# A four-layer graph kernel: half of the zero counts in the second attention loop, ten run-ahead steps stored in mask halves, diagonals and means in another order

## The chip, the cores and the metric

The kernel runs on one core of a Trainium2 chip. The core has a matrix engine (PE), a vector engine (DVE), an activation engine (ACT), a general engine (POOL), and an engine that here only issues transfers (SP). The metric is the device time of one execution, in microseconds, as the median over runs. Beside it stand one profiled execution and its span, from its first to its last instruction.

## The reference

Four residual layers follow one another on 3327 nodes of 64 features, with one 0/1 adjacency matrix of about 0.5 % ones:

```python
h = relu(layernorm(x)); x = x + L0(h, adj)   # hyperbolic attention
h = relu(layernorm(x)); x = x + L1(h, adj)   # decay sum
h = relu(layernorm(x)); x = x + L2(h, adj)   # signed attention with two GRU cells
h = relu(layernorm(x)); x = x + L3(h, adj)   # hyperbolic attention

# L0, L3: adj_att = sigmoid(left + right.T) * adj
#         support = einsum('ij,ijd->id', adj_att, logmap(x_i, x_j)), then expmap and proj
# L1:     rank = cumsum(adj != 0, axis=1); deg = rank[:, -1:]; k = min(deg, 100)
#         pos = rank - (deg - k)
#         out = (mask * where(pos > 0, 0.5 ** (k - pos), 0)) @ (h @ weight) + bias
# L2:     A = adj without its diagonal
#         edge = gru([(A > 0) @ h, (A < 0) @ h], h)
#         node = gru(gat(h, A, A), h)
#         out = diag(adj) * edge + diag(adj) * node
```

In L1 a neighbour counts by how many neighbours stand to its right in the row, so each block of the matrix needs counts before its sum can be made. L2 needs degrees without the diagonal.

## The kernel before

The nodes are padded to 3328, 26 blocks of 128. The matrix lies transposed in memory as f32. The kernel turns it into fp8 masks, thirteen tiles `mask` of two blocks each, and these stay on chip from the first loop to the end. A "quarter" k (0 to 51) is one column half c = k // 26 of one row block b = 25 − k % 26, 128 × 1664 values. Quarters are the unit of loads, masks and zero counts.

The fast path is only right for a matrix of zeros and ones. Therefore each quarter is also read for its zeros (`zeros`, L1335: one DVE instruction that compares with zero and accumulates the result into a column of `zo`). The counts of zeros and ones together must give 3328². The sum of `zo` goes into `ok` (L1964), and after everything else a slow path is taken if the total is wrong.

**First attention (layer 0) and second attention (layer 3), `hyperbolic_series`, L335.** 104 tiles of 1024 or 768 columns are gone through in pairs, index j in a loop at L682. For one tile PE makes two products (L609, L610), ACT takes an arctangent (L615) and a sigmoid (L596), POOL multiplies with the adjacency (L598: in the first loop from f32 as it is loaded, in the second from the masks), DVE makes the weights (L619), PE sums (L628, L636). In the first loop the class `Ahead` (L1316) adds to each j from 2 to 49 one DVE instruction on 128 × 832 values: either half a mask (L1326) or half a zero count (L1335), for quarters 0 to 11 (`EARLY` = 12), with their loads. The second loop has nothing of this kind.

**Decay sum (layer 1), `plain_decay`, L1360.** It goes through the quarters as 52 steps. For a step PE makes counts from the mask (L1437), ACT turns them into weights (`weights`, L1443, an exponential, 128 × 832 at a time, two a step), and PE makes the sums with the two fp16 parts of the features (L1451). The features only become known when the first attention has been finished off on DVE and ACT: `factors` (L709 and after; its tanh is L748, first used at L749), then a layer norm by four groups of blocks (`norms`, L1490 to L1525). During that time counts and weights of the steps 0 to `LAG` − 1 run ahead (`ahead_of_norm`, L1579), with the weights kept in places that are free: halves of masks not yet made, three own tiles and two spare load buffers. Then the loop from L1633 makes the sums of the steps that ran ahead (catching up, at most two sums a step) and counts and weights of the rest.

Masks of the quarters 12 to 51 are made here: `make_mask` (L1421) on DVE for some (L1423) and as a cast on POOL for others (L1426). `check` (L1428) makes the zero count for the quarters that are not in `LATE`, and then issues the load of a further quarter into the buffer that has become free (L1411, on SP). In program order the checks of quarters 16 and later come after the norms.

**Signed attention and GRU (layer 2), `plain_gat`, L1716.** PE goes through 26 blocks (L1738, 16 matmuls each), accumulating in four banks. Between them stand: the last part of layer 1's output (`last_x`, L1269 on PE, addition L1464 on DVE), the layer norm of its last blocks (`finish`, L1545 to L1572), transposes of the features (`turn`, L1774, with five ACT copies each), the diagonal's part of the degrees (`diagonal`, L1786, product L1790, subtraction on DVE L1803), the inverse of the degrees (`inverse`, L1805, ACT and DVE), and a product of weight matrices (`weights2`, L1765). Which of these follows which block is written down in the table `todo`. The nine zero counts of `LATE` are also here, with their own loads (L1753). After the last block the GRU takes the sums out of PSUM (`take`, L1837: ACT copies L1840, DVE multiplication by the inverse degrees L1841) and goes through eight steps (two cells, four column groups) of products, sigmoids and tanhs. An output bank is one half of a PSUM slot; four slots `cnt[0]`, `cnt[1]`, `acc[0]`, `acc[1]` give the banks 0 to 7.

[...]

Of the kernel before, what the change touches and what calls it, by code (L numbers as in the profile page):

```python
# [17 lines left out]
I32 = mybir.dt.int32  # L18
PSUM = bass.MemoryType.PSUM

N = 3327
P = 128
T = 26
# [25 lines left out]
def tile_gnn4(ctx: ExitStack, tc: tile.TileContext, x, adjT, att0, b0, w1, bias1, w_gat, a_gat,  # L49
# [285 lines left out]
    def hyperbolic_series(r, params, ok, masks=None, done=None, ahead=None, then=None):  # L335
# [18 lines left out]
        with ExitStack() as st:  # L354
# [12 lines left out]
            if ahead is not None:  # L367
                ahead.begin(pers)
            lp = st.enter_context(ExitStack())
# [312 lines left out]
            for j in range(-1, K // 2 + (5 if then is None else 1)):  # L682
                for k in (2 * j - 2, 2 * j - 1):
                    if 0 <= k < K:
                        sums(k)
                for i in range(2):
                    k = 2 * j + i
                    products(2 * j + 3 + i)
                    if 0 <= k < K:
                        weights(k)  # L690
                    if i == 0 and (j, 0) in later:
                        later.pop((j, 0))()
                    products(2 * j + 4)
                    if k + 2 < K:
                        angle(k + 2)
                    if k + 3 < K:
                        if masks is None and k + 5 < K:
                            load(k + 5)
                        sigmoid(k + 3)
                    if i == 1 and (j, 1) in later:  # L700
                        later.pop((j, 1))()
                if at(2 * j + 10, 1):
                    columns(at(2 * j + 10, 1))
                if ahead is not None:
                    ahead.step(j)
                if then is not None and j == K // 2 - 1:
                    table_of(AF.Exp)
# [566 lines left out]
    BY_V = range(EARLY + 7, 2 * T - 4, 4)  # L1274
    LATE = *range(EARLY, EARLY + 4), *BY_V[:2], *BY_V[5:]

# [56 lines left out]

    def zeros(same, adj, count):
        V.tensor_scalar(same, adj, 0.0, 0.0, op0=OP.is_equal, op1=OP.add, accum_out=count)  # L1335
# [24 lines left out]
    def plain_decay(e, right, masks, zo, wt, bias, gru, ball_of_r, then):  # L1360
# [8 lines left out]
        LAG = 12  # L1369
# [6 lines left out]
        with ExitStack() as st:  # L1376
# [13 lines left out]
            def in_mask(k, q):  # L1390
                return masks[k].bitcast(BF)[:, q, :].rearrange("p (o h i) -> p o h i", o=2, h=2)

            def in_adj(t, q):
# [3 lines left out]
            places = [in_mask(k, q) for k in (4, 3, 2, 1, 0) for q in range(2)] + own + [  # L1397
                in_adj(t, q) for t in spares for q in range(2)] + [in_mask(0, 0)]

            def place(k):  # L1400
                return places[k] if k < LAG + 6 else in_adj(spares[0], 0) if k == LAG + 9 else own[k % 3]

# [18 lines left out]
            def make_mask(k):  # L1421
                if k in (EARLY, EARLY + 1, EARLY + 4, EARLY + 5, EARLY + 6) or k in BY_V:
                    V.tensor_scalar(mask_of(masks, k), adjs[k], 1.0, None, op0=OP.is_equal, saturate=False)  # L1423
                else:

                    G.tensor_copy(mask_of(masks, k), adjs[k], saturate=False)  # L1426

            def check(k):  # L1428
                if k not in LATE:
                    zeros(same, adjs[k], zo[:, k:k + 1])  # L1430
                buf = adjs.pop(k)
                if k < T + 9 or not any(buf is t for t in ah_.own):
                    load(next(coming), buf)

# [148 lines left out]
            for k in range(EARLY, EARLY + 4):  # L1583
                make_mask(k)
            for k in range(EARLY, EARLY + 4):
                check(k)
# [3 lines left out]
            for k in range(4):  # L1590
                ahead_of_norm(k)
            ah, am = e.factors(tp)
            for k in range(4, LAG):
# [3 lines left out]
            def norms():  # L1597
# [9 lines left out]
                make_mask(EARLY + 4)  # L1607
                rest_of(normed(g, xs[2]))
                make_mask(EARLY + 5)
# [5 lines left out]
                make_mask(EARLY + 6)  # L1615
                centre(groups[3])
                make_mask(EARLY + 7)
# [15 lines left out]
            for k in range(LAG, K_ + 1):  # L1633
# [29 lines left out]
                if k in (LAG + 9, LAG + 11):  # L1663
                    load(next(coming), spares[(LAG + 11 - k) // 2])
                if k == LAG + 5:
                    for i in range(EARLY + 4, k + 1):
                        check(i)
                if EARLY + 8 <= k + LEAD < K_:
                    make_mask(k + LEAD)
                if LAG + 5 <= k < K_ - 1:  # L1670
# [45 lines left out]
    def plain_gat(masks, zo, deg, first, wg, gru, H, parts, banks, last_x, finish, close):  # L1716
# [8 lines left out]
        with ExitStack() as st:  # L1725
# [15 lines left out]

            block(0)
            last_x(0)
            block(1)
# [4 lines left out]
            wk = st.enter_context(room(name="pgl", bufs=4))  # L1749
            late = []  # L1750
            for k in LATE:
                late.append(wk.tile([P, 2, CW], F32, name="adj"))
                nc.sync.dma_start(late[-1], quarters(k))  # L1753
# [8 lines left out]
            for _ in range(1):  # L1762
                before = st.enter_context(ExitStack())
                tp = before.enter_context(room(name="pgn", bufs=1))
                def weights2():  # L1765
                    pt = bank(4)
                    PE.transpose(pt[:D, :D], wg, ident[:D, :D])
                    A.activation(wgT, pt[:D, :D], AF.Copy)
                    pt = bank(5)
# [4 lines left out]
                def turn(t0):  # L1774

                    n = min(4, C2 - t0)
                    pt = bank(4 + t0 // 4 % 2)
# [8 lines left out]
                def diagonal(k):  # L1786

                    dg = bank(6 + k % 2)[:, :BK]
                    for o in range(2):
                        PE.matmul(dg[o * D:(o + 1) * D, :], ones_bf[:, :D],  # L1790
                                  diag[:, o * HP + k * BK:o * HP + (k + 1) * BK], start=True, stop=True)
                    return dg

                def check(n=1):
                    for _ in range(n):
                        same = wk.tile([P, 2, CW], BF, name="same", bufs=1)
                        k = LATE[len(LATE) - len(late)]
                        zeros(same, late.pop(0), zo[:, k:k + 1])

                def degrees(*ks):  # L1800
                    for k in ks:
                        cs = slice(k * BK, (k + 1) * BK)
                        V.tensor_sub(deg[:, cs], deg[:, cs], diagonal(k))  # L1803

                def inverse():  # L1805

                    few, r0 = [tp.tile([P, HP], F32, name=n) for n in ("few", "r0")]
                    V.tensor_scalar(zo[:, 2 * T:2 * T + 2], zo[:, 2 * T:2 * T + 2], first, None, op0=OP.mult)
# [5 lines left out]
                    check(3)  # L1814
                    V.scalar_tensor_tensor(deg, deg, -1.0, r0, op0=OP.mult, op1=OP.mult)
                    V.scalar_tensor_tensor(deg, deg, 2.0, r0, op0=OP.add, op1=OP.mult)
                    check(len(late))


                todo = {11: lambda: (turn(0), check(3)), 12: lambda: degrees(0, 1), 13: lambda: turn(4),  # L1820
                        15: lambda: turn(8), 16: lambda: degrees(2, 3), 17: lambda: (turn(12), inverse()),
                        21: weights2}
# [14 lines left out]
                def take(k):  # L1837
                    cs = slice(k * BK, (k + 1) * BK)
                    for o in range(2):
                        A.activation(xh[0][o][:D, cs], acc[k][o * D:(o + 1) * D, :], AF.Copy, scale=1.0 / SH)  # L1840
# [60 lines left out]
                take(0)  # L1901
                for u in range(K + 2):
                    if u < K:
                        products(u)
                    if u == 0:
                        take(1)
                    if u < K:
                        sigmoids(u)
                    if u == 0:
                        take(2)  # L1910
                        take(3)
# [24 lines left out]
    zo = const.tile([P, 2 * T + 2 + EARLY], F32, name="zo")  # L1936
# [4 lines left out]
    with ExitStack() as ms:  # L1941
# [22 lines left out]
        V.reduce_sum(ok[:, 1:2], zo, axis=AX.X)  # L1964
        rs.close()
        mid.close()
        hyperbolic_series(r3, params3, ok[:, 2:3], masks, store)
# [57 lines left out]
```

## Time and profile before

| | us |
|---|---|
| median of 3 runs | 750.83 |
| lowest, highest | 748.64, 752.13 |
| profiled execution | 747.64 |
| its span | 745.9 |
| mean granted PE clock | 0.951 of full speed |

Busy time by part of the program, from the profile (stretch in us, busy us of PE, DVE, ACT and POOL, granted clock of PE, GB/s moved):

| stretch | PE | DVE | ACT | POOL | clock | GB/s |
|---|---|---|---|---|---|---|
| 250–275, decay, run-ahead | 23.15 | 17.91 | 22.28 | 0.00 | 0.94 | 72 |
| 275–300, decay, norms | 22.60 | 23.05 | 12.83 | 1.70 | 0.93 | 35 |
| 300–316, decay | 11.82 | 10.32 | 5.54 | 7.27 | 0.79 | 259 |
| 316–370, decay | 52.72 | 49.82 | 42.23 | 43.82 | 1.00 | 327 |
| 370–393, decay, end | 20.33 | 15.90 | 15.63 | 15.35 | 1.00 | 168 |
| 393–416, signed attention | 22.11 | 13.78 | 5.51 | 0.00 | 1.00 | 162 |
| 416–444, signed attention | 23.50 | 19.32 | 15.25 | 0.09 | 0.94 | 143 |
| 444–484, GRU | 25.33 | 32.13 | 21.18 | 1.26 | 0.80 | 1 |
| 511–717, second loop | 202.33 | 109.80 | 177.73 | 170.69 | 1.00 | 10 |

The span holds five parts: the first attention to about 247, the decay sum to 393.4, the signed attention to 443.7, the GRU to about 484, and the second attention to the end. An engine whose busy time almost fills its stretch sets the pace there; where none does, the chain of waits names what was waited for. A line of that chain gives the start and the length of a piece and the engine and line that it was spent on.

### The profile page before, as it was taken

To read this page: it belongs to the slowest core of one execution; us is meant where nothing else is said; L and a number is where in the kernel's file an instruction comes from. 1 tells how busy PE (TensorE), PEld (TensorE's weight loads), DVE (VectorE), ACT (ScalarE), POOL (GpSimd) and SP (SyncE) were. 2 spreads that over 40 slices of the span, in tenths; PEclk is the share of its full clock that TensorE was granted. 3 is DMA by queue.
4 is the path that set the end of the run, shared out by engine and by line. 5 is a ranking of instruction groups with operands and counts; after the bars stand their busy time and mean duration, and the time that the engine had idled before them with its cause. 6 is when DMAs were issued, how large, how long until landed. Compare 5 with 4: busy or idle time off the path is not lost.

```text
span 745.9 us, 11819 instructions
## 1 busy us (share of the span) xinstructions
PE 639.6 (86%) x4227; PEld 256.0 (34%) x4227; DVE 521.0 (70%) x922; ACT 538.5 (72%) x693; POOL 466.3 (63%) x353
## 2 busy tenths in 40 slices
PE   0799999999999789799989888229999999999950
PEld 0522233333333333245436542124223333333310
DVE  6857777777777699689875588896555555555556
ACT  2788888888888784387862558167888888889841
POOL 2699989999999100478860000036888788887830
PEclk9999999999999999899999999659999999999995
DMA  3998898998888501699742620001001001000001
GB/s 62 331 274 276 262 291 243 280 290 256 283 248 269 190 1 45 230 358 377 271 142 78 245 92 1 0 0 39 1 2 39 1 1 39 1 0 1 1 3 50
DMA packets 56213, 103.91 MB, mean 139 GB/s; under 512 B 8880, under 2 KB 33104, under 8 KB 56144
## 3 DMA queue, kind: packets, MB, share of 16 engines
q1 hardware_dynamic: 51792, 103.04, 42.3%
q10 hardware_dynamic: 4352, 0.02, 0.3%
q8 instruction: 35, 0.57, 0.3%
q14 instruction: 34, 0.28, 0.1%
HBM read 100.31 MB, written 0.88 MB: 136 GB/s over the span
## 4 chain that ended last, share of the span: by engine, by line
PE 51%; DVE 17%; DMA 10%; ACT 6%; issue 6%; POOL 6%; SPq 2%; ACTq 1%; POOLq 0%; DVEq 0%
PE slot L628 15%; PE slot L636 8%; PE slot L609 8%; DMA adj<-in 7%; PE slot L610 7%; POOL sig L598 6%; PE slot L1437 5%; PE slot L1451 3%; DVE same L1335 3%; PE slot L1738 2%; ACT sig L596 2%; DMA own<-in 2%; DVE sig L619 1%; DVE X L1490 1%; DVE mask L1423 1%
## 5 line engine op out<-in xcount | busy, mean ns | idle before, releaser
L619 DVE SCALAR_TENSOR_TENSOR sig<-slot,sig 128x768 f32<-128x768 f32 (+1 forms) x208 | 212.8, 1023 | 145.5 <-POOL sig L598 142.5
L615 ACT ACTIVATE slot<-slot 128x768 f32<-128x768 f32 (+1 forms) x208 | 177.3, 852 | 54.6 <-PE slot L610 54.5
L598 POOL TENSOR_TENSOR sig<-adj,sig 128x768 f32<-128x768 f32 (+1 forms) x104 | 201.2, 1961 | 14.1 <-ACT sig L596 9.7
L596 ACT ACTIVATE sig<-leftB,right 128x768 f32<-128x768 f32 (+1 forms) x208 | 203.1, 976 | 0.1
L598 POOL TENSOR_TENSOR sig<-mask,sig 128x768 f32<-128x768 fp8e4 (+1 forms) x104 | 173.2, 1676 | 40.4 <-ACT sig L596 35.1
L628 PE MATMUL slot<-sig,Xr 128*64 128x384 f32 (+1 forms) x832 | 169.7, 526 | 6.6 <-DVE sig L619 6.4
L609 PE MATMUL slot<-XC,XT 128*128 128x384 f16 (+1 forms) x416 | 142.2, 342 | 2.8 <-ACT sum L646 1.7
L610 PE MATMUL slot<-XF,XE 73*128 73x384 f16 (+1 forms) x416 | 141.4, 340 | 0.0
L636 PE MATMUL slot<-sig,X 128*32 128x384 f32 (+1 forms) x832 | 94.2, 525 | 0.0
L1443 ACT ACTIVATE w<-slot,ebias 128x832 bf16<-128x832 f32 x72 | 65.4, 951 | 20.7 <-PE slot L1437 20.2
L628 PEld LDWEIGHTS slot<-sig,Xr 128*64 128x64 f32 x832 | 49.5, 135 | 88.6 <-issue 61.3
L609 PEld LDWEIGHTS <-XT 128*128 128x128 f16 x416 | 40.6, 98 | 93.8 <-issue 67.4
L1437 PE MATMUL slot<-mask,rest 128*128 128x416 fp8e4 x208 | 55.8, 351 | 8.2 <-ACT w L1443 3.9
L1437 PE MATMUL slot<-mask,after 128*128 128x416 fp8e4 x208 | 55.3, 349 | 4.2 <-POOL mask L1426 4.2
L610 PEld LDWEIGHTS <-XE 73*128 73x128 f16 x416 | 40.8, 98 | 29.3 <-issue 5.2
L1335 DVE TENSOR_SCALAR_CACHE_REDUCE same<-adj 128x1664 bf16<-128x1664 f32 x25 | 47.0, 1882 | 3.7 <-DMA adj<-in 3.3
L1426 POOL CAST mask<-adj 128x1664 fp8e4<-128x1664 f32 x14 | 22.0, 1570 | 31.2 <-DMA adj<-in 31.2
L1738 PE MATMUL slot<-mask,own 128*64 128x416 fp8e4 x416 | 40.4, 350 | 0.4 <-DVE deg L1461 0.4
L636 PEld LDWEIGHTS slot<-sig,X 128*32 128x32 f32 x832 | 16.4, 108 | 67.7 <-issue 66.1
L1426 POOL CAST mask<-own 128x1664 fp8e4<-128x1664 f32 x7 | 12.7, 1817 | 40.4 <-PE slot L1451 39.6
L419 POOL MEMSET X<- 128x832 f32 x2 | 1.6, 791 | 55.5 <-DVE same L1335 55.5
L1451 PE MATMUL slot<-w,h 128*64 128x416 bf16 x288 | 33.6, 357 | 0.0
(323 smaller groups left out, 678.4 us busy)
## 6 DMA issues: line engine op xcount, KB each, us to landing
adj<-in SPq DMA_DIRECT2D x78, 384.0 KB, 4.8
adj<-in SPq DMA_DIRECT2D x25, 832.0 KB, 7.8
adj<-in SPq DMA_DIRECT2D x27, 512.0 KB, 4.9
ahead<-in SPq DMA_DIRECT2D x12, 832.0 KB, 5.4
ahead<-in SPq DMA_DIRECT2D x16, 416.0 KB, 5.5
own<-in SPq DMA_DIRECT2D x16, 416.0 KB, 5.7
own<-in SPq DMA_DIRECT2D x8, 832.0 KB, 7.5
leftB<-left SPq DMA_DIRECT2D x6, 384.0 KB, 3.6
```

The costliest lines, as they stand in the source:

```text
L596: A.activation(sig, leftB[c], AF.Sigmoid, bias=right[:, b:b + 1])
L598: G.tensor_tensor(sig, adj, sig, op=OP.mult)
L609: PE.matmul(L[:, o, :c[1] * P], XT[:, rows], XC[c][:, o, :], start=True, stop=False)
L610: PE.matmul(L[:, o, :c[1] * P], XE[:KE, rows], XF[c][:, o, :], start=False, stop=True)
L615: A.activation(L, L, AF.Arctan, scale=PA / SX ** 2)
L619: V.scalar_tensor_tensor(sig, slot[:, :, :tiles[k][0][1] * P], PC, sig, op0=OP.add, op1=OP.mult)
L628: PE.matmul(acc[c][o * D:(o + 1) * D, 0, :n], Xr[:, b, :], sigs[k][:, o, :], start=b == 0, stop=b == T - 1)
L636: PE.matmul(acc[c][q:q + 32, 1, :n], X0[:, b - 1 + i, :], w[:, o, :], start=b == 1, stop=b == T - 1, tile_position=(0, q))
L1335: V.tensor_scalar(same, adj, 0.0, 0.0, op0=OP.is_equal, op1=OP.add, accum_out=count)
L1437: PE.matmul(cnt[o][:, h, :BK], w, cols(k, o, h), start=w is after and steps[k][1] == T - 1, stop=True, skip_group_check=True)
L1443: A.activation(ws[k][:, o, :, :], cnt[o][:, :, :BK], AF.Exp, scale=-LN2, bias=ebias)
L1451: PE.matmul(acc[c][o * D:(o + 1) * D, h, :BK], parts[i][:, b, :], w[:, o, h, :], start=b == T - 1 and i == 0, stop=b == 0 and i == 1)
```

## The change

- `LATE` now holds 24 quarters (12 to 19 and 36 to 51). Their zero counts are made in the second attention's loop by a new class `Late`: as 48 half counts of 128 × 832, one for each j from 0 to 47, each with a load of 416 KB issued on SP four steps ahead. The quarters 20 to 35 (`CHECKED`) are counted in the decay sum as before. None is counted in the signed attention. `zo` grows by 24 columns, and its reduction into `ok` comes after the second attention.
- POOL makes its masks by a comparison with one and a multiplication by 0x38 into bytes (the fp8 code of 1.0), in place of a cast. The masks that DVE makes are 12, 13, 16 to 19 and every fourth from 23 to 47.
- `LAG` is 10. The weights that run ahead are kept in the spare load buffers (steps 0 to 3), in the unused halves of the masks 7 to 12 (4 to 9), in the own tiles (10 to 12), again in four of the mask halves (13 to 16), then in the own tiles in turn.
- The masks 12 to 19 pass their buffers to the next loads as soon as each is made. The factors of the norm, with the tanh, are emitted after two run-ahead steps instead of four. The two spare buffers are loaded at steps 13 and 14.
- In the signed attention the diagonals 0 and 1 follow `last_x(0)`, diagonal 2 follows block 3, diagonal 3 and the inverse follow block 4, in other banks; the weight product is split and moved; the transposes follow blocks 12, 14, 16 and 18.
- At the start of the GRU the takes and the multiplications by the inverse degrees are ordered differently, and one take is made by DVE.

```diff
-    BY_V = range(EARLY + 7, 2 * T - 4, 4)
-    LATE = *range(EARLY, EARLY + 4), *BY_V[:2], *BY_V[5:]
+    BY_V = EARLY, EARLY + 1, *range(EARLY + 4, EARLY + 8), *range(EARLY + 11, 2 * T - 4, 4)
+    CHECKED = range(EARLY + 8, EARLY + 24)
+    LATE = [k for k in range(EARLY, 2 * T) if k not in CHECKED]
...
+    class Late:
...
+        def begin(self, pool):
+            self.adjs = [pool.tile([P, CW], F32, name=f"late{k}") for k in range(4)]
+            self.same = pool.tile([P, CW], F8, name="same")
+
+        def load(self, n):
+            if n < 2 * len(LATE):
+                nc.sync.dma_start(self.adjs[n % 4], quarters(LATE[n // 2])[:, n % 2, :])
+
+        def step(self, j):
+            if j < 0:
+                for n in range(4):
+                    self.load(n)
+            if 0 <= j < 2 * len(LATE):
+                k = LATE[j // 2] if j % 2 == 0 else 2 * T + 2 + EARLY + j // 2
+                zeros(self.same, self.adjs[j % 4], self.zo[:, k:k + 1])
+                self.load(j + 4)
+
     def zeros(same, adj, count):
-        V.tensor_scalar(same, adj, 0.0, 0.0, op0=OP.is_equal, op1=OP.add, accum_out=count)
+        V.tensor_scalar(same, adj, 0.0, 0.0, op0=OP.is_equal, op1=OP.add, accum_out=count, saturate=False)
...
-        LAG = 12
+        LAG = 10
...
-            places = [in_mask(k, q) for k in (4, 3, 2, 1, 0) for q in range(2)] + own + [
-                in_adj(t, q) for t in spares for q in range(2)] + [in_mask(0, 0)]
+            places = [in_adj(t, q) for t in spares for q in range(2)]
+            places += [in_mask(k) for k in range(T // 2 - EARLY // 2, T // 2)] + own
+            places += places[4:8]
...
-                if k in (EARLY, EARLY + 1, EARLY + 4, EARLY + 5, EARLY + 6) or k in BY_V:
+                if k in BY_V:
                     V.tensor_scalar(mask_of(masks, k), adjs[k], 1.0, None, op0=OP.is_equal, saturate=False)
                 else:
-                    G.tensor_copy(mask_of(masks, k), adjs[k], saturate=False)
+                    G.tensor_scalar(mask_of(masks, k).bitcast(U8), adjs[k], 1.0, ONE_F8, op0=OP.is_equal, op1=OP.mult)
...
+            def mask_only(k):
+                make_mask(k)
+                check(k)
...
             for k in range(EARLY, EARLY + 4):
-                make_mask(k)
-            for k in range(EARLY, EARLY + 4):
-                check(k)
+                mask_only(k)
+            ahead_of_norm(0)
             for _ in range(3):
                 later.pop(min(later))()
             acc[1] = slots.pop(0)
-            for k in range(4):
-                ahead_of_norm(k)
+            ahead_of_norm(1)
             ah, am = e.factors(tp)
-            for k in range(4, LAG):
+            for k in range(2, LAG):
                 ahead_of_norm(k)
...
-                if k in (LAG + 9, LAG + 11):
-                    load(next(coming), spares[(LAG + 11 - k) // 2])
-                if k == LAG + 5:
-                    for i in range(EARLY + 4, k + 1):
-                        check(i)
+                if k in (LAG + 3, LAG + 4):
+                    load(next(coming), spares[k - LAG - 3])
                 if EARLY + 8 <= k + LEAD < K_:
                     make_mask(k + LEAD)
-                if LAG + 5 <= k < K_ - 1:
+                if EARLY + 8 <= k + 1 < K_:
                     check(k + 1)
...
             block(0)
             last_x(0)
+            for k in range(2):
+                degrees(k, 6 + k)
             block(1)
             last_x(1)
             block(2)
             finish()
...
-                todo = {11: lambda: (turn(0), check(3)), 12: lambda: degrees(0, 1), 13: lambda: turn(4),
-                        15: lambda: turn(8), 16: lambda: degrees(2, 3), 17: lambda: (turn(12), inverse()),
-                        21: weights2}
+                todo = {3: lambda: degrees(2, 4), 4: lambda: (degrees(3, 5), inverse()),
+                        11: lambda: weights2(6), 12: lambda: turn(0, 7),
+                        14: lambda: turn(4, 4), 16: lambda: (weights3(6), inverse2(), turn(8, 5)), 18: lambda: turn(12, 7)}
...
-                take(0)
+                for k in (2, 3):
+                    mean(k)
+                for k in (0, 1):
+                    take(k)
+                take(3, V)
+                for k in (0, 1):
+                    mean(k)
+                take(2)
                 for u in range(K + 2):
                     if u < K:
                         products(u)
-                    if u == 0:
-                        take(1)
-                    if u < K:
                         sigmoids(u)
-                    if u == 0:
-                        take(2)
-                        take(3)
```

## The prediction

> **What bounds the kernel now.** I read the page first, then the chain of waits in the windows where its slices show TensorE (PE) under 9 tenths or at a lower clock, then the timelines of single engines there. From the page:
>
> ```profile
> span 745.9 us, 11819 instructions
> PE   0799999999999789799989888229999999999950
> PEclk9999999999999999899999999659999999999995
> PE 51%; DVE 17%; DMA 10%; ACT 6%; issue 6%; POOL 6%; SPq 2%; ACTq 1%; POOLq 0%; DVEq 0%
> ```
>
> Both attention loops (slices 2 to 12 and 28 to 38) keep PE at 9 tenths and more; no edit shortens their PE work. The loss lies in slices 13 to 27: the decay layer (about 247 to 394 us), the gat layer with its GRU (to 484 us), and the opening of the second attention layer. In the decay layer, the chain of waits:
>
> ```profile
> 256.19 0.22 ACT th L748
> 256.44 0.20 DVE th L749
> ...
> 270.04 0.42 DVE h L1525
> ...
> 300.26 1.81 DVE same L1335 x2
> 302.09 5.01 DMA adj<-in
> 307.15 1.58 POOL mask L1426
> 308.78 0.85 PE slot L1437 x2
> ```
> ```profile
> 366.76 5.01 DMA ahead<-in
> ...
> 372.74 1.89 DVE same L1335 x2
> 374.62 1.33 DVE own L1567
> ...
> 376.40 0.95 ACT w L1443
> 377.39 1.71 PE slot L1437 x8
> ```
>
> Three stalls are seen. The tanh L748 stands behind evictions on ACT; the whole norm on VectorE (DVE) follows it. Then a zero count (L1335), which alone lets its buffer be loaded anew, comes only after the norms: load, POOL mask and counts follow in series. Last, a late load holds up a mask, a count and a piece of norm on DVE, and behind them ACT's evictions. In the gat layer, PE's timeline (start, busy, line, count, idle before):
>
> ```profile
> 417.42 0.37 PE L1790 MATMUL slot<-diag,ones_bf 128*64 128x416 bf16 x2 [1.88 <-DVE deg L1803]
> 425.91 0.37 PE L1790 MATMUL slot<-diag,ones_bf 128*64 128x416 bf16 x2 [0.68 <-DVE deg L1803]
> 427.88 5.82 PE L1738 MATMUL slot<-mask,own 128*64 128x416 fp8e4 x64
> 436.10 0.54 PE L1771 MATMUL slot<-gw,wgT 64*64 64x192 f32 x2 [2.23 <-ACT wgT L1768]
> 436.57 7.50 PE L1738 MATMUL slot<-mask,own 128*64 128x416 fp8e4 x64
> ```
>
> The second diagonal product waits until DVE has read the first, since both lie in one PSUM slot. The same 64 matmuls take 5.82 us before a wait and 7.50 after one.
>
> [...] after the 4.18 us of idle before 308.78: the sums L1451 start at 309.56, 312.58 and 315.06, while a catch-up half step elsewhere takes 1.635. So a PE stall costs more than its length. [...] L1423 beside POOL's cast is 1.9 us instead of 1.02, and the counts L1335 stretch nobody.
>
> **The change part by part**, against the profiled execution (747.64 us, span 745.9; the runs' median is 750.83).
>
> 1. The tanh stands behind four run-ahead evictions instead of eight. On ACT's timeline before, the fourth (250.93, 0.95) ends at 251.88, after t is ready (250.38), so DVE goes on at about 251.9 instead of 256.44: −4.5. Its 14.0 us from there to the first h (270.46) are unchanged, so h comes at 265.9. The remaining 16 run-ahead evictions (L1443, 0.953) end at 251.9 + 16×0.953 = 267.2, beside it. First sum about 267.0 instead of 271.49: −4.5. The following wait for group 1 (277.94 to about 281) is DVE's norm again and stays.
>
> 2. Masks 12 to 19 free their buffers right after being made, without a count, so loads 17 to 24 no longer wait for 300. The stall goes: the three half steps from 303.25 to 315.06 took 11.81 against 3×1.635, −6.9 (4.18 idle, 2.7 slow clock).
>
> 3. With 15 fewer counts in this layer (31 to 16, 1.97 each with its accumulator) DVE is not late at 372; PE's wait there, 373.83 to 379.03 against the regular 2.335 a step, goes: −2.9.
>
> 4. Ten run-ahead steps instead of twelve: two more steps have their counts after the norms, 2×1.505 = 3.0 (four sets of two matmuls each, 0.376). +3.0.
>
> 5. POOL's masks become compare-and-multiply to bytes. The trace has one two-operation tensor_scalar and the casts:
>
> ```profile
> L65 POOL TENSOR_SCALAR offdiag<-ident x1: 293/293/293, 10.8 to 10.8; 128x128 f32<-128x128 f32 x1
> L1426 POOL CAST mask<-adj x14: 1565/1569/1576, 307.2 to 384.1; 128x1664 fp8e4<-128x1664 f32 x14
> ```
> A cast of 128x128 takes 284 beside the 293, so I take 1.6 us a mask and no cost. [...] Upper bound: the two-input rate of L598, 1825 ns for 768, that is 3.95 us for 1664. POOL also has a diagonal and a drop for each second-half step (0.31 + 0.41), under a step of 2.335; three steps in four have a mask on POOL, so 2.15 is free.
>
> Decay: −4.5 −6.9 −2.9 +3.0 = −11.3; its last sum comes at about 381.1 instead of 392.47.
>
> 6. Gat. The nine counts and loads leave DVE and SP. PE's own work from block 0 (393.36) to the last block (443.65) is 50.3 less 1.88, 0.68, 2.23 and about 1.7 of slow clock: 43.8. But the new order has waits of its own. Counted from block 0: diagonal(1) stands right behind diagonal(0) in one slot, and DVE reads it only after the addition L1464 (0.69): about 1.0 of wait, and the second L1269 and all of the norm that follows come 1.65 later. Diagonals 2 and 3 now stand behind blocks 3 and 4, again two banks of one slot. PE reaches diagonal(3) at about +11.8. Its bank comes free when DVE has subtracted diagonal(2), and that subtraction stands on DVE behind the norm: second addition at about +8, chain of 8.4 (399.69 to 408.05 before), subtraction 0.59: +17.2. Queued behind the waiting matmul are all later blocks: a wait of 5.4, and 2.3 of slow clock (between the 1.7 after 2.23 and the 2.7 after 4.18). 43.8 + 1.0 + 5.4 + 2.3 = 52.5: +2.2. Below: were the subtraction in time, 43.8 + 1, so −5.5.
>
> 7. GRU. L1841 and L1840 no longer alternate on ACT and DVE (0.66 a wait on ACT, 2.04 on PE at 450.91). The first products need means 2 and 3, now at the head of DVE. nn of the first steps starts 6.2 and 9.3 after the last block rather than 9.05 and 12.4: −3.0; from there DVE is busy to 483.7 both times.
>
> 8. Loop 2. 48 half counts with 48 loads of 416 KB through SP. Loop 1 shows the price, since it carries a count or a mask in each of 48 pairs (its groups):
>
> ```profile
> L619 DVE SCALAR_TENSOR_TENSOR sig<-slot,sig 128x768 f32<-128x768 f32 x71 | 67.8, 955 | 29.7 <-POOL sig L598 28.4 <-ACT sum L646 1.1
> L1335 DVE TENSOR_SCALAR_CACHE_REDUCE same<-ahead 128x832 bf16<-128x832 f32 x12 | 12.1, 1009 | 0.0
> ```
> A pair of tiles takes 3.65 us (4.71 with 1024 columns) in both loops, with the count as without. Of 3.65, DVE has two L619 and a count, 0.95 + 0.95 + 1.01 + 0.08, leaving some 0.65. The loads are 20 MB over 200 us, 97 GB/s where loop 1 moves about 270. Cover: ACT and PE, the pace-setters. Cost 0; at most +1, as nothing is taken away it cannot gain; without that slack, rival (d). SP's loads of leftB queue behind at most four such loads; loop 1's chunk changes (4.29 to 4.52) equal loop 2's. The ok reduction (0.22) goes to loop 2's end, beside the tail.
>
> Sum: −11.3 + 2.2 − 3.0 = −12.1. Profiled 735.5; on the median scale 750.83×735.5/747.64 = 738.7.
>
> **The rivals.** (a) No gat wait: the subtraction is in time; −7.7 more: 731. For it: 1.10 and 0.53 of the norm's chain are DVE waiting for ACT, so the norm may close up. Against: in the changed program's order the subtraction follows the whole norm on DVE, and the 1.88 before shows that PE waits for such a reader. (b) The decay layer finds a new wait: DVE now makes six of the masks 12 to 19 beside the norms (five before), and with two steps less of cover group 1 or a load is waited for; half of its gain is lost, 744 to 746. For it: the wait at 277.94 shows no slack there. (c) Slower: POOL's masks cost 3.95. POOL makes 25 of them in the loop, 98.8 + 26×0.72 = 117.5; starting at about 280 when mask 20's buffer has landed, the last sum comes near 400.4 instead of 392.47: +7.9 −0.8, some 755 profiled, 758. It decides from about 3.7 us a mask. Against: the 293 ns. (d) Loop 2's counts show: if each stretched its pair by 0.2, 48×0.2 = +9.6: 748, no change. Against: loop 1.
>
> **How the numbers follow.** This measurement can tell about 0.5% from no change, 3.75 us. Chances: forecast 0.50, (a) 0.15, (b) 0.17, (c) 0.08, (d) 0.10. Faster: 0.50 + 0.15 + 0.13 of (b) + 0.02 of (d) = 0.80; within: 0.03 + 0.06 = 0.09; slower: 0.08 + 0.01 + 0.02 = 0.11. Range 729 to 748: it takes in (a), (b) and the edge of (d), and leaves out (c).
>
> **What would show it.** In the chain, th L748 at about 251.6 and the first sum near 267; no stall of PE over 1 us between 285 and the last sum near 381; POOL masks at 1.6; PE idle 5 us before a diagonal product behind block 4, waiting for a DVE subtraction; loop 2 at 3.65 a pair. Wrong if POOL's masks exceed 3 us, if loop 2 takes over 209, or if the gat stall is missing.

## The result and the profile after

| | before | changed |
|---|---|---|
| median, us | 750.5 (748.64 to 752.13, 4 runs) | 832.68 (831.67 to 836.2, 4 runs) |
| ratio to before, 95 % interval | | 1.1104 (1.1062 to 1.1146) |
| span of the profiled execution | 745.9 | 829.9 |
| granted PE clock | 0.951 | 0.91 |

The changed kernel is 11 % slower; 738.7 had been forecast. The page of the changed kernel, in the order of the lines shown of before, with POOL's row and its group of mask instructions besides:

```profile
span 829.9 us, 11980 instructions
...
PE   0899999999985784985666579961899999999970
...
POOL 3799999899994059999999900000688888888840
...
PEclk9999999999998896997877689985899999999995
...
PE 47%; DVE 20%; POOL 17%; issue 6%; ACT 6%; DMA 3%; ACTq 1%; SPq 0%; POOLq 0%; DVEq 0%
...
L1456 POOL TENSOR_SCALAR mask<-adj 128x1664 uint8<-128x1664 f32 x12 | 70.6, 5886 | 20.8 <-DMA adj<-in 19.9
```

POOL's share of the chain has gone from 6 % to 17 %, and a mask on POOL takes 5.89 us where the cast took 1.57. The decay layer has become long and the rest has not, as the stages show. The stages are lengths between the starts of first and last matmuls of a line, which every trace gives:

| stage, us | before | changed |
|---|---|---|
| end of loop 1 to last decay sum | 150.3 | 235.7 |
| signed attention, first to last block | 50.3 | 51.1 |
| last block to start of loop 2 | 67.5 | 64.8 |
| loop 2 | 206.0 | 206.0 |
| tail | 28.7 | 28.5 |

In the decay layer two things are to be seen. The first is the chain of waits in the changed kernel from 364 us on, where one POOL mask follows another:

```profile
363.46 0.82 PE slot L1471 x4
...
364.30 5.82 POOL mask L1456
...
370.19 1.06 POOL mask L206
...
371.33 5.80 POOL mask L1456
...
379.37 6.46 POOL mask L1456
...
386.98 5.82 POOL mask L1456
```

From there to the end of the layer a mask, a diagonal or a drop on POOL is on the chain nearly always: POOL is busy for 109.3 of the 116 us from 364 to 480, PE for 73.4, at a granted clock of 0.75. The second is earlier, in the norm. These are the timelines of POOL and of DVE in the changed kernel:

```profile
290.98 5.81 POOL L1456 TENSOR_SCALAR mask<-adj 128x1664 uint8<-128x1664 f32 x1 [19.91 <-DMA adj<-in]
...
307.95 5.80 POOL L1456 TENSOR_SCALAR mask<-ahead 128x1664 uint8<-128x1664 f32 x1
```
```profile
291.05 5.75 DVE L1530 TENSOR_SCALAR ln_s<-ln_s 128x4 f32<-128x4 f32 x1
...
307.98 5.80 DVE L1542 TENSOR_SCALAR ln_v<-ln_v 128x9 f32<-128x9 f32 x1
```

A DVE instruction on 9 values a partition, 0.17 us long in the run with the cast below, starts just after POOL's mask and ends with it: 5.80 us for a tiny instruction in the series on which the sums wait. The zero counts, which write their accumulator, show nothing of the kind: none of this layer took over 1.89 us, POOL's masks beside them or not. The same happens at the end of the first loop, and there it costs most: two POOL masks, on POOL's timeline, and two DVE masks, on the chain of waits, stand beside one another.

```profile
242.29 12.37 POOL L1456 TENSOR_SCALAR mask<-own 128x1664 uint8<-128x1664 f32 x2
```
```profile
243.11 12.42 DVE mask L1454 x2
```

The two DVE masks took 3.80 in the kernel before, beside two casts that took 3.89. The first sum came at 278.9, and the sums of the last group of blocks at 327.0, against 267.0 and 303.3 in the run with the cast. Counted from the end of loop 1, the way to the last group's sums is 22.8 us longer than there, and the way from these to the last sum, on which POOL sets the pace, 69.6: together the 92.4 between the two layers.

### The profile page after: what moved, and what is told of

Same layout as the page of the kernel before. It is cut to its first block, busy times and chain, and to the rows that moved or that the text cites. A ratio compares the mean times of both kernels' runs of the same rounds, so it can differ in the third digit from the quotient of the medians.

```text
span 829.9 us, 11980 instructions
## 1 busy us (share of the span) xinstructions
PE 664.4 (80%) x4227; PEld 262.9 (32%) x4227; DVE 572.2 (69%) x972; ACT 538.2 (65%) x691; POOL 583.9 (70%) x353
## 4 chain that ended last, share of the span: by engine, by line
PE 47%; DVE 20%; POOL 17%; issue 6%; ACT 6%; DMA 3%; ACTq 1%; SPq 0%; POOLq 0%; DVEq 0%
PE slot L632 14%; POOL mask L1456 11%; PE slot L640 8%; PE slot L613 7%; PE slot L614 6%; PE slot L1767 5%; POOL sig L602 4%; DMA adj<-in 3%; PE slot L1471 3%; DVE mask L1454 2%; ACT sig L600 2%; PE slot L1485 2%; DVE X L1524 1%; POOL mask L206 1%; ACT slot L619 1%
## 5 line engine op out<-in xcount | busy, mean ns | idle before, releaser
L1477 ACT ACTIVATE w<-slot,ebias 128x832 bf16<-128x832 f32 x76 | 70.3, 953 | 109.5 <-PE slot L1471 109.5
L1471 PE MATMUL slot<-mask,after 128*128 128x416 fp8e4 x208 | 63.7, 395 | 42.6 <-POOL mask L1456 42.6
L1456 POOL TENSOR_SCALAR mask<-adj 128x1664 uint8<-128x1664 f32 x12 | 70.6, 5886 | 20.8 <-DMA adj<-in 19.9
L1471 PE MATMUL slot<-mask,rest 128*128 128x416 fp8e4 x208 | 63.3, 392 | 15.0 <-ACT adj L1477 9.8
L1485 PE MATMUL slot<-w,h 128*64 128x416 bf16 x304 | 43.8, 421 | 11.2 <-DVE h L1557 7.1
L1456 POOL TENSOR_SCALAR mask<-own 128x1664 uint8<-128x1664 f32 x7 | 41.3, 5903 | 11.1 <-DVE ns L130 10.6
L1365 DVE TENSOR_SCALAR_CACHE_REDUCE same<-late 128x832 fp8e4<-128x832 f32 x48 | 48.4, 1009 | 0.0
L1456 POOL TENSOR_SCALAR mask<-ahead 128x1664 uint8<-128x1664 f32 x8 | 47.1, 5892 | 0.7
L1471 PEld LDWEIGHTS <-after 128*128 128x128 bf16 x208 | 22.6, 109 | 67.1 <-issue 55.9
```

The costliest lines, as they stand in the source:

```text
L1456: G.tensor_scalar(mask_of(masks, k).bitcast(U8), adjs[k], 1.0, ONE_F8, op0=OP.is_equal, op1=OP.mult)
L1471: PE.matmul(cnt[o][:, h, :BK], w, cols(k, o, h), start=w is after and steps[k][1] == T - 1, stop=True, skip_group_check=True)
L1477: A.activation(ws[k][:, o, :, :], cnt[o][:, :, :BK], AF.Exp, scale=-LN2, bias=ebias)
L1485: PE.matmul(acc[c][o * D:(o + 1) * D, h, :BK], parts[i][:, b, :], w[:, o, h, :], start=b == T - 1 and i == 0, stop=b == 0 and i == 1)
```

## The experiments

Theory P: only POOL's compare-and-multiply was priced wrongly, and the rest of the forecast's sum holds. Rivals: the new order loses by itself (R), or loop 2 or the GRU pays (S). Ratios are to the kernel before on the same chip, with 95 % intervals; a dash stands where the kernel ran only once.

| run | ratio | loop 1 to last sum | blocks | last block to loop 2 |
|---|---|---|---|---|
| cast | 0.9893 (0.9856 to 0.993) | 143.3 | 51.5 | 66.6 |
| before_pool | 1.1386 (1.1351 to 1.142) | 252.3 | 50.3 | 66.4 |
| gat8 | 0.9854 (0.9805 to 0.9902) | 141.3 | 46.8 | 66.0 |
| mulmul | 0.9883 (0.9852 to 0.9915) | 141.2 | 51.1 | 66.3 |
| gat_first | 0.9859 (0.9825 to 0.9893) | 140.2 | 49.2 | 64.7 |
| norm_first | 0.9888 (0.9852 to 0.9923) | 139.9 | 51.9 | 64.7 |
| th_late | 0.9896 (0.9847 to 0.9944) | 142.0 | 51.6 | 64.7 |
| late_counts | 0.9918 (0.989 to 0.9946) | 144.5 | 51.1 | 66.3 |
| take_old | 0.9895 (0.9845 to 0.9945) | 140.1 | 51.2 | 66.6 |
| best | 0.9796 (0.9757 to 0.9835) | 140.1 | 46.0 | 64.7 |
| pool_forms, pool_pairs | – | | | |

Loop 2 took 206.0 in all of them. The runs cast, gat8, mulmul, gat_first and take_old have the same order in the decay layer, with a POOL mask of about 1.6 us, and differ there by 3.2 us: that is what single traces of this stage can't tell apart. The five traces show where the 3.2 comes from. PE waits 3.14 to 3.19 us for group 1 in each, and then runs slowly for a while that differs (the sums of the steps 4 to 16 took 21.4 to 23.1 us); and the last group is waited for in two of them (1.40 and 0.63).

**The cast back (cast).**

```diff
-    G.tensor_scalar(mask_of(masks, k).bitcast(U8), adjs[k], 1.0, ONE_F8, op0=OP.is_equal, op1=OP.mult)
+    G.tensor_copy(mask_of(masks, k), adjs[k], saturate=False)
```

> The changed kernel with POOL's masks made by the cast of before; all else as changed. Theory P, only POOL's compare-and-multiply was mis-sized: the rest of the forecast's sum holds, casts at 1.57 us, last decay sum near 381, about 738.7 us (735 to 742). Rival R, the new order of the decay layer loses time of its own: 745 to 770, with waits of PE over 1 us left between the first and the last sum. Rival S, loop 2 or the GRU pays: the decay layer is short but the total over 745.

Measured 739.32 us, 748.33 for the kernel before beside it. P holds in the total, and the time of the changed kernel falls by some 90 us with this one line. R and S, as the cause of the loss, fall. P's "last sum near 381" does not hold: it was 386.0. The waits that were left, PE's timeline in this run:

```profile
276.79 0.37 PE L1485 MATMUL slot<-mask,h 128*64 128x416 bf16 x2 [3.16 <-DVE h L1557]
...
303.30 0.72 PE L1485 MATMUL slot<-w,h 128*64 128x416 bf16 x6 [1.40 <-DVE h L1559]
```

Group 1 of the norm (the groups are counted from 0 to 3) is waited for, as before, and the last group, 3, now too.

**The same line alone, in the kernel before (before_pool).** The diff is the reverse of the last one, on the old order.

> The kernel before with one line changed: POOL's masks by the compare-and-multiply to bytes. Theory P: the whole loss of the change is this line, on the old order too: 750.5 plus about 90, 825 to 855 us, POOL's masks at 5.8 us each and the chain of the decay layer on POOL. Rival R, the new order has a large part in it: under 800.

Measured 851.21 us. The line is enough for the whole loss, and the old order would have lost more with it: its decay layer is 16.6 us longer than the changed kernel's.

**What is slow about the line (pool_forms).** Nine instructions on 128 × 1664 f32 values of zeros, with a strip of ones:

```diff
+    G.tensor_scalar(pu, pf, 1.0, ONE_F8, op0=OP.is_equal, op1=OP.mult)   # L1850, pu bytes
+    G.tensor_scalar(pu, pf, 1.0, ONE_F8, op0=OP.mult, op1=OP.mult)       # L1851
+    G.tensor_scalar(pu, pf, ONE_F8, None, op0=OP.mult)                   # L1852
+    G.tensor_copy(pu, pf)                                                # L1853
+    G.tensor_scalar(pb, pf, 1.0, ONE_F8, op0=OP.is_equal, op1=OP.mult)   # L1854, pb bf16
+    G.tensor_scalar(pw, pf, 1.0, ONE_F8, op0=OP.is_equal, op1=OP.mult)   # L1855, pw f32
+    G.tensor_scalar(pw, pf, 1.0, ONE_F8, op0=OP.mult, op1=OP.mult)       # L1856
+    G.tensor_scalar(pw, pf, 1.0, None, op0=OP.is_equal)                  # L1857
+    G.tensor_scalar(pw, pf, ONE_F8, None, op0=OP.mult)                   # L1858
```

> As the run with the cast, and nine extra POOL instructions on 128x1664 f32 in the signed attention, whose outputs nobody reads: compare-and-multiply and multiply-multiply to bytes, one multiply and a copy to bytes, compare-and-multiply to bf16 and to f32, multiply-multiply, one compare and one multiply to f32. If the comparison is what costs: every compare near 5 us or more, every multiply under 2.5. If the byte output costs: all four byte outputs near 5 or more, f32 outputs under 2.5. If the second operation costs: only two-operation forms are slow. The cast to fp8 took 1.57.

POOL's timeline of this run (start and length in us):

```profile
380.78 5.86 POOL L1850 TENSOR_SCALAR pu<-pf 128x1664 uint8<-128x1664 f32 x1
386.72 1.58 POOL L1851 TENSOR_SCALAR pu<-pf 128x1664 uint8<-128x1664 f32 x1
388.38 4.42 POOL L1852 TENSOR_SCALAR pu<-pf 128x1664 uint8<-128x1664 f32 x1
392.86 1.57 POOL L1853 CAST pu<-pf 128x1664 uint8<-128x1664 f32 x1
394.50 5.83 POOL L1854 TENSOR_SCALAR pb<-pf 128x1664 bf16<-128x1664 f32 x1
400.40 6.74 POOL L1855 TENSOR_SCALAR pw<-pf 128x1664 f32<-128x1664 f32 x1
407.22 1.58 POOL L1856 TENSOR_SCALAR pw<-pf 128x1664 f32<-128x1664 f32 x1
408.88 4.42 POOL L1857 TENSOR_SCALAR pw<-pf 128x1664 f32<-128x1664 f32 x1
413.38 4.41 POOL L1858 TENSOR_SCALAR pw<-pf 128x1664 f32<-128x1664 f32 x1
```

None of the three guesses is right. The type of the output does not matter (5.86 to bytes, 5.83 to bf16). Neither does the number of operations: a single multiplication, 4.42, costs nearly three times the pair of multiplications, 1.58. What matters is which pair it is. The 6.74 of the comparison to f32 is not a price of the output either, as far as the trace goes: DVE began an instruction with two inputs (L1583, 1.09 us) at 400.38, just before it, and without that 1.09 some 5.7 is left, close to the usual 5.8. That is an inference; the next run has an `is_equal` pair to f32 at 5.86.

**Which pairs are fast (pool_pairs).** The same place, with other pairs, sizes and data: `is_equal`+`add` (L1850), `mult`+`add`, `add`+`mult`, `max`+`min`, `is_gt`+`mult`, `mult`+`max`, `mult`+`is_equal` (L1851 to L1856), and others.

> As the run with the cast, and twelve extra POOL instructions in the signed attention, whose outputs nobody reads, f32 to f32. After the run of forms (multiply-multiply 1.58 us, any compare pair near 5.8, any single operation 4.42) two theories. Theory A, arithmetic pairs have a fast body and everything with a comparison or a bypass a slow one: multiply-add and add-multiply 1.6; compare-add, greater-multiply, multiply-compare near 5.8; maximum-minimum and multiply-maximum 1.6 or slow tells which side they are on. Theory B, only multiply first and a multiply or add second is fast: add-multiply slow too. The slow form by 128, 416 and 832 elements goes in proportion (0.45, 1.45, 2.9) if it is paid per element; ones in place of zeros change nothing if it doesn't depend on the data.

```profile
389.40 5.86 POOL L1850 TENSOR_SCALAR pw<-pf 128x1664 f32<-128x1664 f32 x1 [5.03 <-PE slot L1485]
395.35 1.58 POOL L1851 TENSOR_SCALAR pw<-pf 128x1664 f32<-128x1664 f32 x1
397.00 1.58 POOL L1852 TENSOR_SCALAR pw<-pf 128x1664 f32<-128x1664 f32 x1
398.67 6.74 POOL L1853 TENSOR_SCALAR pw<-pf 128x1664 f32<-128x1664 f32 x1
405.49 5.82 POOL L1854 TENSOR_SCALAR pw<-pf 128x1664 f32<-128x1664 f32 x1
411.39 5.82 POOL L1855 TENSOR_SCALAR pw<-pf 128x1664 f32<-128x1664 f32 x1
417.29 5.81 POOL L1856 TENSOR_SCALAR pw<-pf 128x1664 f32<-128x1664 f32 x1
```

Theory A holds: multiply with multiply, multiply with add and add with multiply take 1.58; every pair with a comparison, a maximum or a minimum takes 5.8 or more. The 6.74 of `max`+`min` met the same DVE instruction as before (L1583, here at 398.65). Full of ones the source gave 5.81, so the data do not matter. A single addition took 5.06, with a DVE mask-sized instruction (L1830) still running until 423.98 beside its start at 423.18. The sizes 128, 416 and 832 took 0.65, 3.21 and 3.44 us where proportion gives 0.45, 1.45 and 2.9. DVE ran two instructions with two inputs on 128 × 1664 values beside the last two, from 428.92 to 432.95, so their times are no clean measurement, and the 3.21 is not explained.

**The fast pair in place of the slow one (mulmul).**

```diff
-    ... adjs[k], 1.0, ONE_F8, op0=OP.is_equal, op1=OP.mult)
+    ... adjs[k], 1.0, ONE_F8, op0=OP.mult, op1=OP.mult)
```

> The changed kernel with POOL's masks by multiply-multiply to bytes (times 1, times 0x38), all else as changed. If the pair of operations alone is what cost: as with the cast, 737 to 742 us, masks at 1.6 each. If the byte view of the mask costs beside it: over 750.

Measured 738.34 us, ratio 0.9883, as with the cast; the masks took 1.58 us each. The byte view of the mask costs nothing; one word of the changed kernel, `is_equal` for `mult`, is its 90 us. For values other than zero and one the two forms give different masks.

**PE's wait in the signed attention (gat8).** Behind the cast:

```diff
-    4: lambda: (degrees(3, 5), inverse()),
+    8: lambda: (degrees(3, 5), inverse()),
```

> As the run with the cast, with the fourth diagonal and the inverse behind block 8 instead of block 4 of the signed attention. If PE's wait of 5.20 us is real cost: 5 to 7.7 us less than with the cast alone, some 731. If something later (inverse, GRU) sets the end of that stage: within 1 us of it.

The changed kernel has the wait that was forecast, in PE's timeline:

```profile
489.20 1.57 PE L1767 MATMUL slot<-mask,own 128*64 128x416 fp8e4 x16
495.98 0.56 PE L1775 MATMUL slot<-diag,ones_bf 128*64 128x416 bf16 x2 [5.20 <-DVE deg L1781]
```

The 112 matmuls that follow this product in the program came only behind it, from 496.27. With the diagonal behind block 8 the wait is gone and the stage is 46.8 us instead of 51.5 (51.1 to 51.9 in all runs with the wait; 739.32 and 736.05 us in all, where the intervals of the two ratios overlap). The stage shows the gain, 4.7, a little under what was expected, because another wait came up: 2.36 us, the first transposes behind the weight product.

**The diagonals ahead of the norm (gat_first).** `degrees(2, 4)` and `degrees(3, 5)` straight behind block 2, `inverse` behind block 4.

> As the run with the cast, with the diagonals 2 and 3 straight behind block 2 and ahead of the norm on DVE, the inverse behind block 4. If the subtraction behind the norm was the cause of PE's 5.20: that wait under 1.2, and 5 to 7.5 us less than with the cast, more than the 3.3 of the diagonal at block 8. If DVE's norm then ends later and another instruction waits for it: no better than at block 8.

The 5.20 became 0.68 as expected, but the stage is 49.2, longer than with gat8. PE's timeline of this run:

```profile
410.58 0.77 PE L1821 MATMUL slot<-ident,own 128*128 128x128 f32 x4 [2.24 <-ACT wgT L1808]
411.28 4.52 PE L1767 MATMUL slot<-mask,own 128*64 128x416 fp8e4 x32
```

The transposes (bank 7) and the weight product (bank 6) lie in one slot, and ACT's copy out of the latter stands behind the logarithm and exponential of the inverse. The 32 matmuls behind took 4.52, where later ones took 3.00: PE was slow again behind the wait.

**Mask 16 out of the norm's way (norm_first).** One line of `norms` moved behind `rest_of(normed(g, xs[2]))`.

> As the run with the cast, with DVE's mask 16 behind group 1 of the norm instead of in it. PE waits 3.16 and 0.43 for that group and then runs three half steps at half clock. If that mask (1.02) is on the path: the wait about 1.0 shorter; if its length also decides the clock, some 3 us less in all, else 1.0. If mask 16 is then late for its counts: no gain.

The wait for group 1 fell from 3.16 to 2.36, but the layer's 139.9 lies at the edge of the 140.1 to 143.3 of runs without the edit: not told apart.

**The tanh late again (th_late).** `e.factors(tp)` behind four run-ahead steps, on the cast.

> As the run with the cast, with the tanh behind eight run-ahead evictions again. If its place sets the first sum (step 1): tanh and first sum about 3.8 us later (270.8 rather than 267.0), the last sum as much later. If the sums that follow wait for something else anyway: last sum within 1 us of the run with the cast.

From the end of loop 1 to the first sum 26.8 us instead of 24.3 to 24.4 in the five runs: +2.5. To the last sum 142.0, inside their 140.1 to 143.3. The start is clearly later; that the end is later could not be shown. Part of the delay was made up on the way: the wait for group 1 was 1.97 us in this trace instead of 3.14 to 3.19, and no slow matmuls followed it (eight sums in 0.89 us).

**Counts behind the norms (late_counts).** On the cast, with `make_mask` in place of `mask_only` for the quarters 16 to 18 in `norms`:

```diff
-    CHECKED = range(EARLY + 8, EARLY + 24)
+    CHECKED = *range(EARLY + 4, EARLY + 7), *range(EARLY + 8, EARLY + 24)
...
+                if k == 17:
+                    for i in range(EARLY + 4, EARLY + 7):
+                        check(i)
```

> As the run with the cast, with the zero counts of quarters 16 to 18 back behind the norms, and their buffers free only then, as before (21 quarters are left to loop 2). If counts that come late were the cause of the stall at 304 (step 2): a wait of PE for a mask from about 295 on, of 3 us or more, and a last sum 4 to 7 us later. If the two spare buffers, which are loaded earlier now, cover it: within 1 us.

No wait for a mask came back near 304, so late counts alone do not bring the stall. The layer took 144.5, 1.2 above the longest of the five: not the 4 to 7 of the first case. PE's timeline of this run has a new wait at the change of column half:

```profile
324.77 0.51 PE L1471 MATMUL slot<-mask,after 128*128 128x416 fp8e4 x2 [2.31 <-DVE deg L1495]
```

The late counts put DVE behind (in this trace it makes counts and masks without a gap from 302.25 on), and the degrees wait in its queue. That the spare buffers, loaded at steps 13 and 14, cover the loads is not shown. Which of the two, early release or early spares, took the stall of 304 away is left open: both gone at once was not tried.

**The takes in the old order (take_old).** The order of before, on ACT, on the cast.

> As the run with the cast, with the takes and means of the GRU's start in the order of before, on ACT. If that order is worth 3.0 us (step 7): loop 2 starts 69.5 to 70 us after the last block rather than 66.6. If DVE's later work sets the start of loop 2 anyway: within 1 us of 66.6.

66.6 us against 66.6, by the total no gain. But in DVE's timeline the third nn starts 9.5 us after the last block in the run with the cast, 11.35 in this one and 12.4 in the kernel before. The cast's run gave its 1.85 back in the prologue of loop 2, where DVE waited 0.25 to 0.77 us a time for PE's transposes; gat_first, with the same GRU code as the cast and without most of these waits, has 64.7, and the trace of take_old, without them too, 66.6. So the order of the takes brings about 1.9 up to the third nn. How much of it reaches loop 2 differs: in the nine traces with the new order the stretch took 64.7 to 66.6.

**A version that beats both (best).** mulmul, the diagonals of gat_first, norm_first, and `weights2(4)` in place of `weights2(6)`, so that the weight product and the first transposes lie in different slots.

> The changed kernel with multiply-multiply masks, mask 16 behind group 1 of the norm, diagonals 2 and 3 ahead of the norm in the signed attention, and the weight product's first bank moved to another slot than the first transposes (in the runs with the diagonals moved PE waited 2.2 to 2.4 us for it). If these gains add: about 10 us less than with the cast alone, 729 or below. If the signed attention only hands its wait on again: some 734.

Measured 732.95 us, ratio 0.9796 (0.9757 to 0.9835): about 2 % faster than the kernel before. It is some 6 below the cast, not 10 (739.32 and 732.95 in different sets of runs). The signed attention took 46.0 us, with no wait of PE over 1 us left in it; the 2.24 is gone.

## Why the prediction was wrong

**The step that failed** is the fifth: "A cast of 128x128 takes 284 beside the 293, so I take 1.6 us a mask and no cost." The row of 293 ns was the nearest by name, a tensor_scalar of two operations on POOL. Its line in the kernel is a multiplication and an addition, one of the three fast pairs, and the new instruction's pair is not. Engine, form and number of operations agreed, but not the operations themselves, and on POOL these decided: at the row's own size, 128 × 128, the comparison with a multiplication took 0.65 us (pool_pairs) where the row has 0.293. The upper bound failed too: 3.95 us, the rate of L598's multiplication of two tensors, 1825 ns for 768, was taken as the worst case, and the instruction took 5.80. So the 1.6 and the 3.95 were both built from faster instructions, and the true price lay above both. Divided by the 1664 elements of a partition, as an estimate, the measured 5.80 us are 3.49 ns an element, the 4.42 of the single multiplication 2.66, and the 1.58 of the arithmetic pairs 0.95.

**Rival (c)** had the mechanism, at too low a price: POOL becomes the engine that sets the pace of the decay layer. The picture fits: from 308 to the end of the last POOL mask at 473.1 POOL was busy for 161.3 of 165.2 us. Its own sum with the measured price, 25×5.80 + 26×0.72 = 163.7, comes out the same partly by luck, since only 23 of the 25 masks ran in that time and the rest of POOL's work was more than the 0.72 a step. And it had started the sum at 280, 28 us too early. The mask that starts at 307.95 in the changed kernel starts at 291.40 in the run with the cast, behind an addition that waits for the norm, so some 11 us were missing from the sum at any price of a mask; the other 16.5 are the norm being late, its DVE instructions held up beside POOL's long ones (5.75 and 5.80 us where 0.17 is usual). That effect the prediction named for DVE's masks beside POOL's casts (1.9 us instead of 1.02); for the 5.80 us instruction it was in no sum.

**The other steps**, with POOL's masks at 1.6 us:

- Step 1: first sum 24.3 to 24.4 us after loop 1 instead of 28.8: −4.4, forecast −4.5. That all of it reaches the end was not shown (th_late).
- Step 2: the stall at 304 is gone; in its place group 3 of the norm is waited for, 1.40 in the run with the cast, 0.63 with mulmul, not at all in three runs. Step 3: after 325 no wait of PE over 0.4 us in the run with the cast. Step 4 was not tried by itself.
- The decay layer together: 140.1 to 143.3 in five runs instead of 150.3 in the one trace of before, mean 141.2, so −9.1 where −11.3 was forecast. The waits for groups 1 and 3 cost more than the sum had: it left the wait for group 1 as it was, 2.05, and it became 3.14 to 3.19. Rival (b) named this group, at a larger price; norm_first took 0.8 off the wait by moving one of DVE's masks.
- Step 6: wait of 5.20 (5.4 forecast), stage +0.8 to +1.6 in the runs with it (forecast +2.2). The slow clock afterwards (0.53 granted from 495.9 to 500) was over-priced: 112 matmuls took 11.76 at 496 and 10.04 later, 1.7 us.
- Step 7: −2.9 to the third nn (forecast −3.0), of which the order of takes is 1.85; the other 1.05 were not traced. To the start of loop 2 the gain is −0.9 to −2.8, not −3.0: the forecast let DVE be busy without a break from there, and in the run with the cast it waited for PE's transposes.
- Step 8: 0, as forecast; the line of PE's sums in loop 2, before and after, starts and ends 206.0 us apart with and without 48 counts and loads:

```profile
L628 PE MATMUL slot<-sig,Xr x416: 486/486/643, 511.2 to 717.2; 128*64 128x384 f32 x104, 128*64 128x512 f32 x35
```
```profile
L632 PE MATMUL slot<-sig,Xr x416: 486/486/643, 595.4 to 801.4; 128*64 128x384 f32 x104, 128*64 128x512 f32 x35
```

The ratio forecast, 738.7/750.83 = 0.984, is just under the interval of the run with the cast (0.9856 to 0.993): without the one line the change gains about 1.1 % rather than 1.6 %. That the 739.32 of the cast lies so close to the 738.7 is in part luck: the kernel before took 748.33 in that set of runs, not 750.83, and the parts were off in both directions.

## What to carry to other kernels

A row of the profile prices an instruction only if the operations are the same; here, on POOL, the engine, the shape and the number of operations agreed and the time differed by 3.7 times (1.58 and 5.80 us). An instruction that no row shows should get an upper bound at which the forecast turns, and if that bound (here 3.7 us a mask) is not excluded by a row of just that kind, the case deserves a chance to match. Work could be moved to an engine with measured slack at no cost (48 counts in loop 2, 206.0 us with and without), but two PSUM uses in one slot behind a long queue brought a wait with them (5.20 us at the fourth diagonal, 2.24 at the transposes of gat_first).

## What the runs showed of the hardware

- POOL's tensor_scalar on 128 × 1664 f32: 1.58 us for multiply-multiply, multiply-add and add-multiply, 4.42 for a single multiply or compare, 5.8 for pairs with a comparison or a maximum. A single operation is dearer than a pair of multiplications (one factor being 1.0) that computes the same.
- A POOL instruction of 5.8 us held a DVE tensor_scalar on 4 to 9 values a partition for as long, and two POOL masks in a row stretched two DVE masks to 12.42, where beside two casts they took 3.80. DVE's counts, which write their accumulator, were not stretched (1.89 at most).
- PE was slow behind some waits and not behind others. In the kernel before its granted clock was 0.50 from 309.5 to 312.5, behind a wait of 4.18 us, and 0.53 from 280.1 to 283.6, behind one of 2.05. Behind the 3.16 in the run with the cast, eight sums took 1.60 (at 280.27) where later ones took 0.89, and behind the 2.24 in gat_first, 32 matmuls took 4.52 instead of 3.00. Behind 2.36 (gat8) 32 matmuls took 3.00, and behind 1.97 (th_late) eight sums took 0.89: not slow. So not every stall cost more than its length, and the length of the wait alone did not decide it. How long PE stayed slow behind the same wait (3.14 to 3.19) differed as well, and with it the same decay code (21.4 to 23.1 us for the sums of the steps 4 to 16).
